# Cross-attention with image prompts: a column read in place, a key chunk and a sum moved in the last batch

## The chip, the cores and the metric

The kernel runs on one core of one Trainium2 chip. Its time is device microseconds of one launch, the median of several runs. The core's engines are TensorE (PE in the profile; PEld is its weight load), VectorE (DVE), ScalarE (ACT), GpSimd (POOL) and SyncE (SP), which issues the transfers. Each works through its own queue of instructions in order and waits on semaphores for the others.

## The reference

For 8 batches of 112 queries with 320 channels (20 heads of 16) there are 371 text keys and 4 prompt keys, each a row of 512. The core of what is computed:

```python
q = heads(hidden_states @ W_q); k_t = heads(text_ehs @ W_k); v_t = heads(text_ehs @ W_v)
probs_t = softmax(q k_t * scale);  text_out = probs_t v_t
attn_scores = q k_ip * scale
qsem = l2norm(probs_t @ text_ehs);  sem = qsem @ l2norm(ip_ehs)
probs_ip = softmax(attn_scores + 0.5 * sem) * spatial_mask
out = (text_out + probs_ip v_ip) @ W_out + b_out + hidden_states
```

All is float32.

## The kernel before, in words

The length of qsem isn't taken from qsem itself: with the Gram matrix G of the text rows, its square is p G p. So each batch builds a matrix u (L426, L506) that holds G in blocks of 32 rows, the products with the normalised prompts, a column of ones and the values of the heads at hand. For each head, `multiplied` (L574 on) forms p u in 12 steps j of four matmuls, one for each of the four heads of a group (L587). From the result's PSUM banks, ACT copies the last 21 columns into pvs (`value_sums`, L600): 4 prompt products, the sum of p (column NIP) and 16 value sums. `reduced` (L625) multiplies the first 371 columns by p and sums them on DVE, which gives the squared length, ss. In the last batch two of a group's four heads go another way: `shared` copies the bank on ACT (L610), multiplies on POOL (L614) and sums on ACT (L618).

The heads of a batch are worked on in five groups g = 0 to 4. `scores` (L540) and `probabilities` (maximum on DVE L553, exponential on ACT L557, transfer into the ring xg) run two groups ahead of `multiplied`; `transposed` (L568) turns the ring into xgT one group ahead. `placed` (L506, on POOL) puts the values of the next group's heads into u, in three pieces, each as soon as PE is done with that piece of the group before.

`keys` makes the transposed keys kT in three chunks of 128 channels (L448, copied at L455). Groups 0 and 1 need the first chunk, groups 2 and 3 the second, group 4 the third. In the last batch (b = 7) the third chunk is made after the products of group 1 (L941).

`finish` is a generator that takes a batch from pvs and ss to the output in pieces, so that its pieces can be set between other work: the sum with the bias xb (L659, POOL); z, the sum of p, copied out of pvs (L661), z2 = z * z * eps * eps and rn = max(ss, z2) (L664, L666); the root (L669, between two loads of ACT tables) and attn = values / z (L675, POOL); the fused prompt scores fu (L680 to L686); their exponential ex (L690); sums and weights w (L696 to L700, DVE), and in the same piece the weighted prompt values wv (L702), their fold (L713) and two additions to attn (L714, L715), all four on POOL; the transpose of attn (L721) and its copy aT (L725); the product with W_out (L734); the addition of xb (L743); the transfer out (L746). The last batch is finished in two parts: heads 0 to 15 (`first`) while group 4 is multiplied, heads 16 to 19 (`last`, late=True, on DVE where others use POOL) at the very end. `awake` issues matmuls on a unit matrix whose result nobody reads (ps_w, L371).

The orders of PE, SP, DVE and (after the prologue) ACT are those of the source. POOL's order isn't: a scheduler of the framework decides it at build time, from when it expects operands to be ready. The last batch is written out by hand from L907 to L962. PSUM has three pools: four banks for products (ps_qd), two for scores (ps_sc) and two for the rest (ps_mm), given out in turn; in the last batch heads 0 and 1 of the groups from 2 on take their scores' banks from ps_mm, as the key chunk does.

Of the kernel before, what the change touches and what calls it, by code (L numbers as in the profile page):

```python
# [8 lines left out]
F32 = mybir.dt.float32  # L9
# [5 lines left out]
NIP = 4  # L15
# [5 lines left out]
def kernel(  # L21
# [14 lines left out]
    nc = tc.nc  # L36
# [327 lines left out]
    def awake(n, end=False):  # L364

        if end:
            ps = ps_qd.tile([P, 512], F32, tag="qd", name=f"ps_w_{n}")
        else:
            ps = bank(f"ps_w_{n}", spare=True)
        for _ in range(n):  # L370
            nc.tensor.matmul(ps[:, :P], ident, ident, start=True, stop=True)  # L371
# [266 lines left out]
    def finish(b, heads=(0, H), eng=None, late=False, table=None):  # L638


        s = st[b]
        eng = eng or nc.gpsimd
        h0, h1 = heads
        n = h1 - h0
        part = slice(h0, h1)

        def sm(name):
            return small.tile([S, H], F32, tag=name, name=f"{name}_{b}_{h0}", bufs=1)[:, :n]

        def sm4(name):  # L650
            return small.tile([S, H, NIP], F32, tag=name, name=f"{name}_{b}_{h0}", bufs=1)[:, :n]

        def over_ip(t):
            return t.unsqueeze(2).to_broadcast([S, n, NIP])

        pvs = s["pvs"][:, part]
        if not late:
            s["xb"] = work.tile([S, C], F32, tag="xb", name=f"xb_{b}", bufs=1)
            nc.gpsimd.tensor_tensor(s["xb"], x_sb[:, b, :], bias_sb, ALU.add)  # L659
        z = sm("z")  # L660
        nc.vector.tensor_copy(z, pvs[:, :, NIP])  # L661

        z2 = sm("z2")
        nc.vector.scalar_tensor_tensor(z2, z, EPS * EPS, z, ALU.mult, ALU.mult)  # L664
        rn = sm("rn")
        nc.vector.tensor_tensor(rn, s["ss"][:, part], z2, ALU.max)  # L666
        yield

        nc.scalar.activation(rn, rn, AF.Sqrt)  # L669
        nc.scalar.preload_act_table(AF.Exp)  # L670
        zr = sm("zr")
        nc.vector.reciprocal(zr, z)
        attn = attn_ring[b % 2]
        ah = attn[:, :C].rearrange("p (h d) -> p h d", d=D)[:, part]
        eng.tensor_tensor(  # L675
            ah, pvs[:, :, NIP + 1 :], zr.unsqueeze(2).to_broadcast([S, n, D]), ALU.mult
        )
        yield

        nc.vector.reciprocal(rn, rn)  # L680
        fu = sm4("fu")
        nc.vector.tensor_tensor(fu, pvs[:, :, :NIP], over_ip(rn), ALU.mult)
        nc.vector.scalar_tensor_tensor(fu, fu, SEM_SCALE, s["ipl"][:, part], ALU.mult, ALU.add)
        mx = sm("mx")
        nc.vector.tensor_reduce(mx, fu, AX.X, ALU.max)
        nc.vector.tensor_tensor(fu, fu, over_ip(mx), ALU.subtract)  # L686
        yield

        ex = sm4("ex")
        nc.scalar.activation(ex, fu, AF.Exp)  # L690
        if table:
            nc.scalar.preload_act_table(table)
        yield

        sx = sm("sx")
        nc.vector.tensor_reduce(sx, ex, AX.X, ALU.add)  # L696
        rx = sm("rx")
        nc.vector.reciprocal(rx, sx)
        w = sm4("w")
        nc.vector.scalar_tensor_tensor(w, ex, sm_sb, over_ip(rx), ALU.mult, ALU.mult)  # L700
        wv = work.tile([S, NIP, H, D], F32, tag="wv", name=f"wv_{b}_{h0}", bufs=1)[:, :, :n]
        eng.tensor_tensor(  # L702
            wv,
            s["vip"][:, :, part],
            w.rearrange("p h n -> p n h").unsqueeze(3).to_broadcast([S, NIP, n, D]),
            ALU.mult,
        )
        if late:
            ips = small.tile([S, GROUP, D], F32, tag="ips", name=f"ips_{b}", bufs=1)
            nc.vector.tensor_reduce(ips, wv.rearrange("p n h d -> p h d n"), AX.X, ALU.add)  # L710
            nc.vector.tensor_tensor(ah, ah, ips, ALU.add)
        else:
            eng.tensor_tensor(wv[:, :2], wv[:, :2], wv[:, 2:], ALU.add)  # L713
            eng.tensor_tensor(ah, ah, wv[:, 0], ALU.add)  # L714
            eng.tensor_tensor(ah, ah, wv[:, 1], ALU.add)  # L715
        yield

        i0, i1 = h0 * D // P, -(-h1 * D // P)
        ps = bank(f"ps_a_{b}_{h0}", spare=True)
        for i in range(i0, i1):  # L720
            nc.tensor.transpose(  # L721
                ps[:, i * S : (i + 1) * S], attn[:, i * P : (i + 1) * P], ident[:S, :S]
            )
        aT = work.tile([P, NC, S], F32, tag="aT", name=f"aT_{b}_{h0}")
        nc.scalar.copy(  # L725
            aT[:, i0:i1], ps[:, i0 * S : i1 * S].rearrange("p (i s) -> p i s", s=S)
        )
        yield

        if not late:  # L730
            s["o"] = bank(f"ps_o_{b}", spare=b >= B - 2)
        ps = s["o"]
        for i in range(i0, i1):
            nc.tensor.matmul(  # L734
                ps[:S, :C], aT[:, i, :], wo_sb[:, i, :], start=(i == 0), stop=(i == NC - 1)
            )
        if h1 < H:
            yield
            return
        yield  # L740

        ob = work.tile([S, C], F32, tag="ob", name=f"ob_{b}", bufs=1)
        nc.vector.tensor_tensor(ob, ps[:S, :C], s["xb"], ALU.add)  # L743
        yield

        nc.sync.dma_start(out[b], ob)  # L746
        del st[b]
        yield
# [12 lines left out]
    def run(key, make, pieces=1):  # L761

        if key not in gens:
            gens[key] = make()
        for _ in range(pieces):
            next(gens[key], None)

    def between(b, g):

        nb = b + 1  # L770
        new = nb < B


        first = [bs for bs in pairs if bs[0] == (nb if b == 0 else nb + 1)]
        rest = [bs for bs in pairs if bs[0] == nb]
        if g == 0:
            if new:
                run(("g", nb), lambda: gram(nb), 3)
            if b == 0:
                run(("pp",), prompt_projections, NC + 1)  # L780
            if b > 0:
                run(("f", b - 1), lambda: finish(b - 1))
        if g == 1:
            if new:
                run(("v", nb), lambda: values(nb), 2)
            for bs in first if b == 0 else ():
                run(("q", bs[0]), lambda: project_queries(bs), 3)
        if g == 2 and new:
            run(("v", nb), None)
            run(("k", nb), lambda: keys(nb))  # L790
            for bs in first if b == 0 else ():
                run(("q", bs[0]), None)
        if g == 2 and b > 0 and new:
            run(("f", b - 1), None)
        if g == 3:
            if new:
                run(("k", nb), None, 1)
            for bs in first if b > 0 else ():
                run(("q", bs[0]), lambda: project_queries(bs), 3)
            run(("t", b), lambda: prompt_logits(b))  # L800
            if nb < B - 1:
                run(("k", nb), None, 1)
            if b > 0 and new:
                run(("f", b - 1), None)
            for bs in rest:
                run(("q", bs[0]), None)
        if g == 4:
            if nb + 1 < B:
                run(("c", nb + 1), lambda: transposed_context(nb + 1))
            if b > 0 and new:  # L810
                run(("f", b - 1), None, 2)
            if nb + 1 < B:
                run(("c", nb + 1), None, 2)
            for bs in (first if b > 0 else []) + rest:
                run(("q", bs[0]), None)
# [94 lines left out]
    for g in range(NG):  # L910
# [7 lines left out]
        for j, _ in enumerate(multiplied(b, g)):  # L918
            for a in {0: (2, 3), 1: (0, 1)}.get(j, ()) if g == 0 else ():
                scores(b, coming, a)  # L920
                probabilities(b, coming, a)
            if j == 2 and g + 1 < NG:
                transposed(b, g + 1)
            if j == 2 and g == 1:
                run(before, None, 3)
# [12 lines left out]
            run(("f", b - 2), None)  # L938
        if g == 1:
            prompt_values(b)  # L940
            run(("k", b), None)  # L941
        between(b, g)
        if g == 2:
            run(before, None)
        if g == 3:

            first = finish(b, (0, FULL * HC), table=AF.Sqrt)
            for _ in range(5):
                next(first)
    last = finish(b, (FULL * HC, H), nc.vector, late=True)  # L950
    run(before, None, 2)
    awake(14, end=True)
    for _ in range(3):
        next(last)
    run(before, None)
    next(last)
    next(first)
    next(first)
    run(before, None)
    drain(first)  # L960
    awake(2, end=True)
    drain(last)  # L962


# [41 lines left out]
```

## Time and profile before

| what | value |
|---|---|
| median of 3 runs (lowest, highest) | 456.55 us (455.42, 456.96) |
| the profiled execution: its time, its span | 457.1 us, 455.3 us |
| PE busy | 440.5 us, 97% |
| DVE, ACT, POOL busy | 313.7, 188.8, 113.3 us |
| mean granted clock of PE | 0.991 |
| last batch: first product to last instruction | 401.4 to 455.3 us |

The profile is of one execution. Times in it are us from the start of the span. A row of the timeline gives the start, the duration, the engine, the line and operation, the tile written and the tiles read (numbers left out), their shapes, how many instructions are merged into the row, and in brackets for how long the engine had been idle and what ended that. PEclk is the clock that was granted to PE, as a share of the full one. Each float32 matmul of the source appears as two in the trace.

### The profile page before, as it was taken

What the parts mean: (1) busy time and instruction counts of PE and PEld (TensorE: products, weight loads), DVE (VectorE), ACT (ScalarE), POOL (GpSimd) and SP (SyncE); (2) the same over time, 40 slices, a digit from 0 to 9 for tenths busy, and PEclk for the clock granted to TensorE, in tenths of its full rate; (3) what the DMA queues carried; (4) which work ended last, traced back from release to release, by engine and by line L of the source; (5) the groups of instructions that cost most, each with busy time, mean ns of one, the idle gap of its engine ahead of it and who ended that gap; (6) DMA issues with size and microseconds to landing.
All of it is one profiled execution on the core that took longest, in us unless ns stands there. A gap on an engine that the chain in (4) does not pass through costs nothing. (4 is left out here: it accounts for less than half of the span.)

```text
span 455.3 us, 12992 instructions
## 1 busy us (share of the span) xinstructions
PE 440.5 (97%) x5146; PEld 340.1 (75%) x5146; DVE 313.7 (69%) x670; ACT 188.8 (41%) x523; POOL 113.3 (25%) x262
## 2 busy tenths in 40 slices
PE   8998999999999999999999999999999999998976
PEld 8757867877678877887678777888777877875854
DVE  4047276786677768787686768787686768888854
ACT  2264233345334353345335353435344353346532
POOL 4302200102051113222060212311150212323570
PEclk9999999999999999999999999999999999999989
DMA  8669954645646554545645555545645445654200
GB/s 238 181 167 252 201 134 136 150 128 163 161 125 160 142 139 140 140 138 158 170 119 141 153 156 145 139 125 151 170 125 131 140 114 157 148 146 138 61 1 25
DMA packets 52068, 64.99 MB, mean 143 GB/s; under 512 B 18368, under 2 KB 43984, under 8 KB 52008
## 3 DMA queue, kind: packets, MB, share of 16 engines
q1 hardware_dynamic: 51568, 63.62, 53.1%
q8 instruction: 40, 0.66, 0.7%
q10 hardware_dynamic: 440, 0.56, 0.4%
q14 instruction: 20, 0.16, 0.1%
HBM read 19.46 MB, written 5.12 MB: 54 GB/s over the span
## 5 line engine op out<-in xcount | busy, mean ns | idle before, releaser
L587 PE MATMUL ps_qd<-u,xgT 32*112 32x232 f32 (+11 forms) x3840 | 220.9, 356 | 4.2 <-POOL u L506 3.8
L587 PEld LDWEIGHTS ps_qd<-u,xgT 32*112 32x112 f32 x3840 | 185.0, 173 | 42.4 <-issue 10.9
L553 DVE TENSOR_REDUCE nmx<-ps_s 112x1 f32<-112x371 f32 x160 | 77.6, 528 | 68.7 <-PE ps_s L540 68.0
L568 DVE STREAM_TRANSPOSE xgT<-xg 128x1536 f32<-128x1536 f32 x40 | 118.9, 2972 | 7.3 <-DMA xg<-p 7.3
L557 ACT ACTIVATE p<-ps_s,nmx 112x371 f32<-112x371 f32 x160 | 82.5, 573 | 62.6 <-DVE nmx L553 46.7
L625 DVE CUSTOM_DVE_ANT_0 junk<-ps_qd,p 112x371 f32<-112x371 f32 x154 | 83.5, 542 | 22.5 <-ACT pvs L600 5.7
L506 POOL COPY u<-vr 128x64 f32<-128x64 f32 x120 | 26.1, 240 | 169.4 <-PE ps_qd L587 113.4
L540 PE MATMUL ps_s<-kT,qm 32*112 32x371 f32 x320 | 62.9, 480 | 2.4 <-ACT kT L455 2.1
L465 PE MATMUL ps_v<-wv_sb,ctxT 128*128 128x384 f32 (+1 forms) x192 | 63.5, 480 | 0.0
L465 PEld LDWEIGHTS ps_v<-wv_sb,ctxT 128*128 128x128 f32 x192 | 35.2, 190 | 19.7
L448 PE MATMUL ps_k<-ctxT,wk_sb 128*128 128x371 f32 x144 | 48.7, 482 | 0.0
L600 ACT COPY pvs<-ps_qd 112x21 f32<-112x21 f32 x160 | 16.5, 189 | 72.6 <-PE ps_qd L587 72.6
L448 PEld LDWEIGHTS ps_k<-ctxT,wk_sb 128*128 128x128 f32 x144 | 26.5, 190 | 16.1 <-issue 0.5
L412 PE MATMUL ps_g<-ctxT 128*128 128x375 f32 (+2 forms) x168 | 37.4, 379 | 0.0
L412 PEld LDWEIGHTS ps_g<-ctxT 128*128 128x128 f32 x168 | 28.1, 190 | 8.4
L540 PEld LDWEIGHTS ps_s<-kT,qm 32*112 32x112 f32 x320 | 25.1, 170 | 7.3 <-ACT kT L455 4.7
L310 DVE TENSOR_SCALAR qm<-ps_q,emask 128x224 f32<-128x224 f32 (+1 forms) x25 | 9.2, 400 | 25.1 <-PE ps_q L301 25.1
L702 POOL TENSOR_TENSOR wv<-vip,w 112x1280 f32<-112x1280 f32 (+1 forms) x8 | 19.2, 2405 | 17.0 <-DVE w L700 14.8
L472 ACT COPY vext<-ps_v 128x384 f32<-128x384 f32 (+1 forms) x24 | 11.2, 466 | 24.9 <-PE ps_v L465 24.4
L455 ACT COPY kT<-ps_k 128x371 f32<-128x371 f32 x18 | 8.5, 472 | 27.3 <-PE ps_k L448 27.3
L400 ACT ACTIVATE ug<-ps_g 128x375 f32<-128x375 f32 (+2 forms) x24 | 9.0, 377 | 23.5 <-PE ps_g L412 19.0
L401 POOL TENSOR_TENSOR ug<-ug,half 128x128 f32<-128x128 f32 (+1 forms) x24 | 10.7, 448 | 29.9 <-ACT ug L400 29.9
(111 smaller groups left out, 323.2 us busy)
## 6 DMA issues: line engine op xcount, KB each, us to landing
xg<-p SPq DMA_DIRECT2D x160, 162.3 KB
u<-ug SPq DMA_DIRECT2D x128, 99.0 KB
vip<-vipd SPq DMA_DIRECT2D x8, 560.0 KB
ct<-in_ctx_dram SPq DMA_DIRECT2D x16, 256.0 KB
vr<-vd SPq DMA_DIRECT2D x32, 120.0 KB
vd<-vext SPq DMA_DIRECT2D x7, 320.0 KB
ct<-in_ctx_dram SPq DMA_DIRECT2D x8, 224.0 KB
vd<-vext SPq DMA_DIRECT2D x7, 160.0 KB
```

The costliest lines, as they stand in the source:

```text
L412: nc.tensor.matmul(ps[:, : T - t0], ctxT[:, e, t0 : t0 + P], ctxT[:, e, t0:T], start=(e == 0), stop=(e == NE - 1),)
L448: nc.tensor.matmul(ps[:, :TT], wk_sb[:, e, i * P : (i + 1) * P], s["ctxT"][:, e, :TT], start=(e == 0), stop=(e == NE - 1),)
L465: nc.tensor.matmul(ps[:, :w], ctxT[:, e, c * P : (c + 1) * P], wv_sb[:, e, :w], start=(e == 0), stop=(e == NE - 1),)
L506: nc.gpsimd.tensor_copy(region(b, c)[:, :, UV - c * P :], s["vr"][:, c * QN : (c + 1) * QN, g, :])
L540: nc.tensor.matmul(ps[:S, :TT], qm[a * RG : (a + 1) * RG, i, r, j * S : (j + 1) * S], s["kT"][a * RG : (a + 1) * RG, i, :], start=True, st ...
L553: nc.vector.tensor_reduce(nmx, ps[:S, :TT], AX.X, ALU.max, negate=True)
L557: nc.scalar.activation(p, ps[:S, :TT], AF.Exp, bias=nmx)
L568: nc.vector.transpose(xT.rearrange("p j (k q) -> p q j k", q=QN), xg.rearrange("p q (j k) -> p q j k", k=RG),)
L587: nc.tensor.matmul(banks[a][:S, j * RG : UW], xT[a * RG : (a + 1) * RG, j, :S], region(b, c)[a * RG : (a + 1) * RG, q, q * RG :], start=(j ...
L600: nc.scalar.copy(s["pvs"][:, h, :], ps[:S, TT:UW])
L625: nc.vector.tensor_tensor_reduce(out=junk, in0=ps[:S, :TT], in1=s["p", g][:, a, :], scale=1.0, scalar=0.0, op0=ALU.mult, op1=ALU.add, accu ...
L702: eng.tensor_tensor(wv, s["vip"][:, :, part], w.rearrange("p h n -> p n h").unsqueeze(3).to_broadcast([S, NIP, n, D]), ALU.mult,)
```

## The change

It has five edits, all in the arrangement, none in what is computed.

- In `finish`, z is no longer copied; column NIP of pvs is read in place by z2 and by the reciprocal.
- In the last batch xb takes its memory from the buffers named ctxT (which hold the transposed context and later the tile of `shared`) and not from the single buffer xb.
- `finish` gives up control once more, between w and wv. The calls are adapted: group 2 of other batches runs two pieces where it ran one; for batch 6, w stays at group 2 of the last batch, and wv with what follows is issued after the value columns of group 4.
- The third chunk of the last batch's keys is issued inside the products of group 1, after step j = 1.
- In the tail, 11 keep-awake matmuls replace 14, the last two go, and the transpose of `first` with its copy aT is issued ahead of the exponential ex of `last`.

```diff
         if not late:
-            s["xb"] = work.tile([S, C], F32, tag="xb", name=f"xb_{b}", bufs=1)
+            if b == B - 1:
+                s["xb"] = work.tile([P, NE, TP], F32, tag="ctxT", name=f"xb_{b}")[:S, 0, :C]
+            else:
+                s["xb"] = work.tile([S, C], F32, tag="xb", name=f"xb_{b}", bufs=1)
             nc.gpsimd.tensor_tensor(s["xb"], x_sb[:, b, :], bias_sb, ALU.add)
-        z = sm("z")
-        nc.vector.tensor_copy(z, pvs[:, :, NIP])
+        z = pvs[:, :, NIP]
...
         nc.vector.scalar_tensor_tensor(w, ex, sm_sb, over_ip(rx), ALU.mult, ALU.mult)
+        yield
...
         if g == 2 and b > 0 and new:
-            run(("f", b - 1), None)
+            run(("f", b - 1), None, 2)
...
+            if j == 1 and g == 1:
+                run(("k", b), None)
             if j == 2 and g + 1 < NG:
                 transposed(b, g + 1)
...
         if g == 1:
             prompt_values(b)
-            run(("k", b), None)
         between(b, g)
         if g == 2:
             run(before, None)
         if g == 3:
+            run(before, None)
             first = finish(b, (0, FULL * HC), table=AF.Sqrt)
-            for _ in range(5):
+            for _ in range(6):
                 next(first)
     last = finish(b, (FULL * HC, H), nc.vector, late=True)
     run(before, None, 2)
-    awake(14, end=True)
+    awake(11, end=True)
     for _ in range(3):
         next(last)
     run(before, None)
+    next(first)
     next(last)
-    next(first)
     next(first)
     run(before, None)
     drain(first)
-    awake(2, end=True)
     drain(last)
```

## The prediction

> **What bounds the kernel now.** I read the page first. TensorE (PE) is busy nearly all the time, at full clock but for two slices near the end.
>
> ```profile
> PE 440.5 (97%) x5146; PEld 340.1 (75%) x5146; DVE 313.7 (69%) x670; ACT 188.8 (41%) x523; POOL 113.3 (25%) x262
> PEclk9999999999999999999999999999999999999989
> ```
>
> Every edit that acts before the last batch only shortens VectorE (DVE) there, so the question is the last batch (404 us to the end). The busy times by 1 us stretch (columns: stretch, length, busy PE, PEld, DVE, ACT, POOL, granted clock, DMA) show its two holes:
>
> ```profile
> 418.00:419.00 1.00, 0.00 (x0) 0.00 (x0) 0.75 (x3) 1.00 (x5) 0.40 (x1) 1.00 1.01 297
> 421.00:422.00 1.00, 1.00 (x9) 0.46 (x8) 1.00 (x3) 1.00 (x3) 0.00 (x0) 0.50 0.00 0
> 433.00:434.00 1.00, 0.00 (x0) 0.00 (x0) 0.85 (x3) 0.17 (x1) 0.92 (x2) 1.00 0.00 0
> 438.00:439.00 1.00, 1.00 (x12) 0.69 (x8) 0.76 (x3) 1.00 (x1) 0.00 (x0) 0.50 0.00 0
> ```
>
> PE stands still at 418 and 433, and each time runs at clock 0.50 some microseconds later. The timeline (start, duration, engine, line, tiles) says why:
>
> ```profile
> 409.61 1.00 DVE L661 COPY z<-pvs 112x20 f32<-112x20 f32 x1
> 410.64 0.18 DVE L664 SCALAR_TENSOR_TENSOR z<-z 112x20 f32<-112x20 f32 x1
> 410.95 1.89 DVE L553 TENSOR_REDUCE nmx<-ps_s 112x1 f32<-112x371 f32 x4
> 411.58 1.96 ACT L557 ACTIVATE p<-ps_s,nmx 112x371 f32<-112x371 f32 x4 [2.61 <-POOL shared L614]
> 414.46 2.76 PE L448 MATMUL ps_k<-ctxT,wk_sb 128*128 128x371 f32 x8
> 418.74 0.52 ACT L455 COPY kT<-ps_k 128x371 f32<-128x371 f32 x1
> 419.31 1.05 PE L540 MATMUL ps_s<-kT,qm 32*112 32x371 f32 x8 [2.09 <-ACT kT L455]
> 429.41 2.47 POOL L702 TENSOR_TENSOR wv<-vip,w 112x1280 f32<-112x1280 f32 x1 [0.17 <-DVE w L700]
> 435.32 0.61 POOL L506 COPY u<-vr 128x64 f32<-128x64 f32 x3
> 435.61 6.49 PE L587 MATMUL ps_qd<-u,xgT 32*112 32x392 f32 x96 [2.70 <-POOL u L506]
> ```
>
> First hole, 2.09 us: the third key chunk is made after group 1's products, and its copy kT stands on ACT behind two table loads and group 1's evacuation. Second hole, 2.70 us: the value columns u of group 4 stand on POOL behind wv, its fold and two additions of batch 6. The tail after group 4 (442.10) is a chain too:
>
> ```profile
> 444.77 3.29 PE L371 MATMUL ps_w<-ident 128*128 128x128 f32 x28
> 446.99 0.21 ACT L690 ACTIVATE ex<-fu 112x16 f32<-112x16 f32 x1
> 448.29 0.35 ACT L725 COPY aT<-ps_a 128x224 f32<-128x224 f32 x1 [1.08 <-PE ps_a L721]
> 450.30 0.26 PE L721 MATMUL ps_a<-ident,attn 112*128 112x112 f32 x1
> ```
>
> **What the Trainium skill says.** "TensorE: Matmul & The Clock Gate", Part 1: the clock is halved after an idle activity window of about 3.4 us, and the window runs free, so the same kernel meets it at different phases. The trace agrees: 0.50 from about 420.0 to 423.4 and from 437.0 to 440.3. "SBUF — State Buffer", Who interferes with whom: a DVE instruction with two SBUF inputs and a GpSimd instruction that reads SBUF exclude each other, the later one blocks. The trace agrees: with a POOL multiplication from 155.24 to 155.70, z2 (L664) started at 155.41 and ended at 155.74, 0.33 us in place of 0.18. For the rest no page is needed.
>
> **The change part by part.** All sums are against the profiled execution (457.1 us, span 455.3, so 1.8 us lie around it); it stands 0.55 us above the median of 456.55.
>
> *Score column in place.* Nine copies go. Those of batches 0 to 5 took about 0.17 us each under PE work (58 to 60 us busy in each 60 us stretch): nothing; were that cover gone, 6 x 0.2 = 1.2 us. Batch 6's took 1.00 us at 409.61, since POOL's second multiplication (L614) held the port until 410.58. The next instruction, z2, has two SBUF inputs, so I take it that it now waits there itself until 410.62; only 0.17 + 0.04 = 0.21 us are won for the maxima and exponentials behind it. Other bound: z2 isn't blocked, and the first exponential moves to 410.65, where its own wait for POOL ends: 0.93 us. The first of batch 7 (0.54 us at 434.87) leads to POOL's attention of its heads 0 to 15, ready at 444.01, 3.9 us ahead of its transpose: nothing. The second (0.16 us at 444.89) stands ahead of ex, which gets another wait (below): nothing.
>
> *Third chunk inside the products.* The built order puts its four matmuls behind steps j = 0 and 1 of group 1. The chunk's PSUM bank is the one of scores (group 3, head 0), so it waits for that exponential, the third of four at 0.46 us: 412.50 to 413.07, after the change 412.86. PE gets there at 410.45, where j = 2 started before. So PE waits 2.45 us, with ten steps of group 1 queued behind. Then 2.76 us of chunk and the rest of group 1 (414.46 - 410.45 = 4.01): group 1 ends at 412.90 + 6.77 = 419.67. Scores of group 4, formerly 419.31, start then, 0.36 us later. kT now precedes the table loads on ACT (copy done 416.2, loads, root and exponential 3.3 us more: 419.6), just in time for the evacuation.
> Before, group 2 found its banks long free. Now it starts on group 1's heels, and waits for its copies and sums as group 1 did behind group 0, whose products end at 407.87: from one end to the next 414.46 - 407.87 = 6.59 us. Group 2 ends at 426.26 at full clock; it was 426.48, of which half clock cost 6.36 - (5.71 - 0.42) = 1.07.
> Half clock: about 2.2 us of PE idling inside a 3.4 us window is what both holes before had (2.1), so it likely strikes again, now on the chunk and group 1. Cost between 1.07 (measured on products) and 1.7 (half of 3.4 on dense matmuls); I take 1.5: 427.76, against before +1.28. Without it -0.22.
>
> *Batch 6's sums "behind" the value columns.* They are issued later in the source, but POOL's order isn't written by hand, and in the built program wv, fold and additions still stand ahead of u. The second hole stays whole, with its half clock.
>
> *xb.* It leaves POOL's end (447.20 to 448.06, off the path) for a place between the value columns of group 3 and the multiplications of group 2: it runs 426.97 to 427.83 by the old clock, so these start 0.5 us later than 427.32 and end at 429.78, and wv, waiting for them and for w, starts at about 429.9: +0.5 (bounds 0.39 and 0.55), straight into group 4's start. Its new buffer waits for sums of ACT that ended at 423.9: nothing.
>
> *Tail.* 3 of 14 keep-awake matmuls go: 6 x 0.1175 = 0.70 us, and 0.61 us of the last two. But aT of the first 16 heads now precedes ex on ACT: PE ends ps_w at 447.36, aT takes 447.58 to 447.93, ex ends at 448.19 in place of 447.20, and the chain from it to attn (2.27 us, less 0.15 for xb gone from POOL) at 450.35; the last transpose starts at 450.5, it was 450.30: +0.2 (bounds -0.7, if that chain shrinks as well, and +0.6, if PE cools down while it waits). No DMA is added; SP's order is the same.
>
> Sum: 1.28 + 0.5 + 0.2 = +2.0: 459.1 as profiled, 458.5 beside the median.
>
> **Rivals.** (1) No half clock: the wait straddles two windows. Then -0.22 + 0.5 + 0.2 = +0.5: 457.0, not slower by what can be told. For it: free phase, and runs before that spread over 1.5 us. Against: both holes before struck. It decides below some 1.5 to 2 us of idling in one window. (2) The lock isn't taken: the wait shrinks by 0.72 to 1.7 us, too short for half clock; -0.22 - 0.72 + 0.7 = -0.2: 456.3. Against: z2 at 155.41. (3) The change does what it says on POOL: u right behind group 3, group 4 at 432.9 in place of 435.6, no half clock: -2.7 - 1.1, a later attention of batch 7 gives back 0.5: about 453.5. Against: the built order.
>
> **How the numbers follow.** A measurement of this kernel can tell about 0.3% (1.4 us) from no change: 455.2 to 457.9. Forecast 0.52, nearly all of it above 457.9; rival 1 0.28; rival 2 0.08; rival 3 0.07; something unseen 0.05. Slower 0.50, same 0.38, faster 0.12. The range runs from rival 2 (456.2) to the forecast with the full 1.7 us, xb's upper bound and a cooled tail (459.6), leaving out rival 3 and the unseen. The forecast's own range is 457.5 to 459.6.
>
> **What would show it.** Right: a PE hole of about 2.4 us at 410.5 ahead of ps_k, clock 0.50 behind it, no hole before the scores, wv still ahead of u, the hole of about 3 us before group 4, ex behind aT. Wrong: exponentials of group 3 from 410.7, full clock throughout group 1, or u ahead of wv.

## The result: 459.01 us, 0.55% longer

| kernel | median | lowest, highest | runs | profiled execution: time, span, mean clock of PE |
|---|---|---|---|---|
| before | 456.55 us | 455.42, 457.23 | 9 | 457.1, 455.3, 0.991 |
| after | 459.01 us | 457.33, 459.82 | 9 | 459.82, 458.0, 0.983 |

The ratio is 1.0055, with a 95% interval from 1.0039 to 1.0071. The forecast was 458.5.

The profiled execution of after is the slowest of its nine and one of two with a mean clock of 0.983. Six of the nine had 0.989 or 0.990, hardly less than the 0.991 of before's profiled execution. So the trace of after shows more time at half clock than most of its executions had, and its account must be read with that in mind.

The page of after, its busy times and its clock by slices:

```profile
PE 442.0 (96%) x5136; PEld 339.3 (74%) x5136; DVE 311.4 (68%) x661; ACT 188.4 (41%) x523; POOL 113.1 (25%) x262
PEclk9999999999999999999999999999999999997979
```

PE has ten records less than before and is busy 1.5 us longer: its work did not grow, it ran more slowly. Of the last four slices two stand at 7 in the clock's row; before, the lowest was a single 8. The busy times by 1 us stretch (columns as before) show where:

```profile
411.00:412.00 1.00, 0.00 (x0) 0.00 (x0) 1.00 (x3) 1.00 (x3) 0.00 (x0) 0.88 0.00 0
...
414.00:415.00 1.00, 1.00 (x2) 0.44 (x2) 1.00 (x2) 0.00 (x0) 0.00 (x0) 0.50 0.63 183
...
436.00:437.00 1.00, 0.00 (x0) 0.00 (x0) 0.83 (x3) 0.00 (x0) 0.92 (x2) 0.50 0.00 0
...
440.00:441.00 1.00, 1.00 (x12) 0.60 (x8) 0.54 (x2) 1.00 (x1) 0.19 (x1) 0.50 0.00 0
```

There are still two holes. The first has moved from 418 to 411, the second is at the same place of the program, ahead of group 4. The timeline of after, the rows that answer to those of before:

```profile
409.07 1.00 DVE L667 SCALAR_TENSOR_TENSOR z<-pvs 112x20 f32<-112x20 f32 x1
410.11 0.18 DVE L669 TENSOR_TENSOR rn<-ss,z 112x20 f32<-112x20 f32 x1
410.20 1.89 DVE L553 TENSOR_REDUCE nmx<-ps_s 112x1 f32<-112x371 f32 x4
410.82 1.95 ACT L557 ACTIVATE p<-ps_s,nmx 112x371 f32<-112x371 f32 x4 [2.42 <-POOL shared L614]
...
412.37 5.31 PE L448 MATMUL ps_k<-ctxT,wk_sb 128*128 128x371 f32 x8 [1.64 <-ACT p L557]
...
417.72 0.47 ACT L455 COPY kT<-ps_k 128x371 f32<-128x371 f32 x1 [3.96 <-PE ps_k L448]
...
421.43 0.86 PE L540 MATMUL ps_s<-kT,qm 32*112 32x371 f32 x8
...
428.41 0.87 POOL L663 TENSOR_TENSOR xb<-x_sb,bias_sb 112x320 f32<-112x320 f32 x1
...
431.32 2.47 POOL L707 TENSOR_TENSOR wv<-vip,w 112x1280 f32<-112x1280 f32 x1 [0.18 <-DVE w L703]
...
437.23 0.64 POOL L506 COPY u<-vr 128x64 f32<-128x64 f32 x3
...
437.54 7.22 PE L587 MATMUL ps_qd<-u,xgT 32*112 32x392 f32 x96 [3.13 <-POOL u L506]
```

Read it from the bottom of the first hole: the key chunk (ps_k) is released by an exponential (p, L557), not by its operands, and its eight matmuls take 5.31 us where they took 2.76. Row z is now the instruction z2 itself, and it takes the 1.00 us that the copy took. The scores no longer wait for kT. On POOL wv still stands ahead of u, and group 4 still waits for u, longer than before, and then takes 7.22 us where it took 6.49. The tail of after:

```profile
447.43 2.62 PE L371 MATMUL ps_w<-ident 128*128 128x128 f32 x22
...
450.28 0.34 ACT L730 COPY aT<-ps_a 128x224 f32<-128x224 f32 x1 [0.82 <-PE ps_a L726]
450.52 0.22 ACT L693 ACTIVATE ex<-fu 112x16 f32<-112x16 f32 x1
...
453.05 0.29 PE L726 MATMUL ps_a<-ident,attn 112*128 112x112 f32 x1 [1.04 <-DVE attn L716]
```

The exponential ex stands behind aT, and the last transpose waits 1.04 us for attn.

Where the 2.7 us between the two spans lie can be added up from the starts of ACT's copies pvs (L600), which follow the end of each group's products at once:

| stretch | before | after | difference |
|---|---|---|---|
| start of the span to the copies of group 0 | 407.81 | 407.26 | -0.55 |
| copies of group 0 to copies of group 2 | 18.65 | 20.70 | +2.05 |
| copies of group 2 to the first product of group 4 | 9.15 | 9.58 | +0.43 |
| group 4, first product to its copies | 6.51 | 7.25 | +0.74 |
| those copies to the end of the span | 13.18 | 13.21 | +0.03 |
| span | 455.3 | 458.0 | +2.7 |

In this execution half clock lasted two stretches of 3.4 us at each hole of the last batch; before had one at each. Of the kernels below that keep the chunk at this place, four had one stretch on it (e2, e6, e7, e9): for them the second row is 19.36 to 19.73, that is +0.7 to +1.1. With the +0.43 of the third row this makes +1.1 to +1.5 for an execution with one stretch at each hole. What else belongs to the 2.46 us between the medians no trace shows.

### The profile page after: what moved, and what is told of

It reads as the page before. It is cut to its first block, busy times and chain, and to the rows that moved or that the text cites. A ratio compares the mean times of both kernels' runs of the same rounds, so it can differ in the third digit from the quotient of the medians.

```text
span 458.0 us, 12965 instructions
## 1 busy us (share of the span) xinstructions
PE 442.0 (96%) x5136; PEld 339.3 (74%) x5136; DVE 311.4 (68%) x661; ACT 188.4 (41%) x523; POOL 113.1 (25%) x262
## 4 chain that ended last, share of the span: by engine, by line
PE 91%; ACT 3%; POOL 2%; DMA 2%; DVE 1%; issue 1%; SPq 0%; DVEq 0%; ACTq 0%
PE ps_qd L587 42%; PE ps_v L465 14%; PE ps_k L448 10%; PE ps_g L412 8%; PE ps_s L540 4%; PE ps_q L301 3%; PE ps_o L739 3%; PE ps_c L351 2%; ACT p L557 1%; PE ps_g L384 1%; DMA xg<-p 1%; PE ps_w L371 1%; DMA ct<-in_ctx_dram 1%; PE ps_a L726 1%; PE ps_ip L517 1%
## 5 line engine op out<-in xcount | busy, mean ns | idle before, releaser
L587 PE MATMUL ps_qd<-u,xgT 32*112 32x168 f32 (+11 forms) x3840 | 221.5, 356 | 4.8 <-POOL u L506 4.3
L557 ACT ACTIVATE p<-ps_s,nmx 112x371 f32<-112x371 f32 x160 | 82.4, 572 | 64.0 <-DVE nmx L553 48.3
L448 PE MATMUL ps_k<-ctxT,wk_sb 128*128 128x371 f32 x144 | 51.3, 502 | 1.6 <-ACT p L557 1.6
L600 ACT COPY pvs<-ps_qd 112x21 f32<-112x21 f32 x160 | 16.4, 188 | 71.5 <-PE ps_qd L587 71.4
L448 PEld LDWEIGHTS ps_k<-ctxT,wk_sb 128*128 128x128 f32 x144 | 27.6, 197 | 19.2 <-ACT p L557 2.2
```

The lines of the kernel that those rows point to most:

```text
L448: nc.tensor.matmul(ps[:, :TT], wk_sb[:, e, i * P : (i + 1) * P], s["ctxT"][:, e, :TT], start=(e == 0), stop=(e == NE - 1),)
L557: nc.scalar.activation(p, ps[:S, :TT], AF.Exp, bias=nmx)
L587: nc.tensor.matmul(banks[a][:S, j * RG : UW], xT[a * RG : (a + 1) * RG, j, :S], region(b, c)[a * RG : (a + 1) * RG, q, q * RG :], start=(j ...
L600: nc.scalar.copy(s["pvs"][:, h, :], ps[:S, TT:UW])
```

## The experiments

The theory to test: the loss is the wait of the chunk for its PSUM bank, with half clock behind it, not the chunk's new place as such, and the other edits give nothing or cost a little. The first rival was that the other edits (xb, the tail) make the loss; the second, that the chunk costs by standing inside the products, wait or no wait. None of these kernels leaves out or changes a part of the computation. "0 to 2" is the stretch from the copies of group 0 to those of group 2, in us, in the profiled execution. The ratios are to runs of before beside them, whose medians were 456.70 to 456.90 us (456.55 for after). They are worked out from the single runs and can differ from the quotient of two medians by up to 0.15%.

| kernel | median | ratio to before, 95% interval | chunk: wait, duration | 0 to 2 | group 4: wait, duration |
|---|---|---|---|---|---|
| before | 456.55 | | none, 2.76 | 18.65 | 2.70, 6.49 |
| after | 459.01 | 1.0055 [1.0039, 1.0071] | 1.64, 5.31 | 20.70 | 3.13, 7.22 |
| e1 chunk back | 456.64 | 1.0012 [0.9992, 1.0032] | none, 2.76 | 16.76 | 3.08, 6.49 |
| e2 chunk alone | 458.63 | 1.0040 [1.0021, 1.0059] | 1.84, 4.45 | 19.73 | 2.69, 6.49 |
| e3 chunk after j = 6 | 455.66 | 0.9977 [0.9965, 0.9989] | none, 2.76 | 16.43 | 3.11, 6.40 |
| e4 other bank | 456.69 | 0.9998 [0.9983, 1.0014] | 0.72, 2.76 | 16.93 | 3.13, 7.59 |
| e5 POOL by hand | 458.38 | 1.0039 [1.0024, 1.0055] | 2.25, 5.32 | 21.28 | 1.13, 7.00 |
| e6 ex first | 457.59 | 1.0013 [0.9997, 1.0030] | 1.65, 4.27 | 19.36 | 3.11, 6.34 |
| e7 xb back | 457.96 | 1.0030 [1.0017, 1.0044] | 1.66, 4.46 | 19.54 | 2.69, 6.49 |
| e8 maxima first | 456.70 | 1.0000 [0.9980, 1.0021] | 0.87, 2.76 | 17.06 | 3.12, 7.41 |
| e9 hole filled | 457.28 | 1.0015 [1.0001, 1.0028] | 1.66, 4.46 | 19.54 | 0.59, 4.80 |
| e10 column alone | 456.43 | 0.9994 [0.9972, 1.0017] | none, 2.76 | 18.52 | 2.69, 6.49 |
| e11 repaired | 453.61 | 0.9924 [0.9900, 0.9947] | none, 2.76 | 15.98 | 0.56, 4.80 |
| e12 repaired, POOL by hand | 453.54 | 0.9933 [0.9911, 0.9955] | none, 2.76 | 15.96 | 0.97, 5.77 |

### Which edit makes the loss

**e1: after, with the chunk back behind the products of group 1.**

```diff
-            if j == 1 and g == 1:
-                run(("k", b), None)
...
             prompt_values(b)
+        if g == 1:
+            run(("k", b), None)
```

> The changed kernel, but the third key chunk stands behind group 1's products again, as before the change. Theory (the chunk's wait on its bank inside group 1 and the half clock behind it make the loss): what remains is xb's 0.43 us in front of wv and up to 0.7 us of half clock in group 4, so 457.0 to 457.8, 0.5 to 1.2 us above before, and a first hole ahead of the scores of about 2 us as before. Rival (xb, the column read in place or the tail make the loss): stays at about 459.0, 2.5 us above before.

**e2: before, with the move of the chunk alone.**

```diff
+            if j == 1 and g == 1:
+                run(("k", b), None)
...
             prompt_values(b)
-            run(("k", b), None)
```

> The kernel before with only the third key chunk moved behind step j = 1 of group 1. Theory: this edit alone makes most of the loss, 1.3 to 2.1 us, so 457.9 to 458.7; PE waits about 2 us ahead of ps_k and the chunk runs at half clock. Rival (the other edits make it): within 0.5 us of before.

The timeline of e2 at the chunk:

```profile
413.58 4.45 PE L448 MATMUL ps_k<-ctxT,wk_sb 128*128 128x371 f32 x8 [1.84 <-ACT p L557]
```

The move alone makes 0.40% [0.21%, 0.59%] of the 0.55%, and with it undone no difference from before can be told. So the chunk is the main part, the other edits together make no difference that can be told, and the first rival falls. e1 came out 0.4 us below what was expected: in its profiled execution the old hole ahead of the scores was there (1.88 us), but no half clock followed it, so that 0 to 2 took 16.76 us and not 18.65.

### The wait, or the place

**e3: after, with the chunk after step j = 6,** where the exponentials of group 3 are done.

```diff
-            if j == 1 and g == 1:
+            if j == 6 and g == 1:
```

> The changed kernel with the chunk behind step j = 6 of group 1 and not j = 1. By then the exponential that frees its bank has ended, so theory: no wait ahead of ps_k, no half clock in group 1; kT stands behind ex on ACT and the scores of group 4 wait about 1 us; group 2 ends about 1.4 us earlier than before, less 0.43 for xb and up to 0.7 for half clock in group 4: 455.5 to 456.3. Rival (a chunk inside the products costs by itself, since group 2 then starts on group 1's heels): 457.5 or more.

**e4: after, with the chunk in a bank of the scores' pool,** which the first and not the third of the four exponentials sets free.

```diff
-            ps = bank(f"ps_k_{b}_{i}")
+            ps = bank(f"ps_k_{b}_{i}", spare=b == B - 1 and i == FULL)
```

> The changed kernel with the chunk's PSUM bank taken from the scores' pool, whose next bank is freed by the first of the four exponentials and not by the third, 0.93 us earlier. Theory: the hole ahead of ps_k shrinks from 1.6 to about 0.7 us, too short for half clock: 455.9 to 456.6; if half clock strikes all the same, about 458. Rival (the wait on the bank is not what costs): stays at about 459.

**e8: after, with the first piece of batch 6's finish (z2 among it) issued behind group 3's maxima,** so that these don't stand behind z2.

```diff
-            if b > 0:
+            if 0 < b < B - 1:
                 run(("f", b - 1), lambda: finish(b - 1))
...
             probabilities(b, coming, a)
+        if g == 1:
+            run(before, lambda: finish(b - 1))
         drain(sums)
```

> The changed kernel with z2 and rn of batch 6 behind the four maxima of group 3 on DVE and not ahead of them. Theory (z2 waits for POOL's multiplications, and the maxima wait behind it): z2 falls from 1.00 to about 0.2 us, the first exponential starts 0.7 us earlier, right when POOL ends, and the hole ahead of ps_k is about 0.9 us and not 1.64; 456.5 to 458.3, by whether half clock still strikes. Rival (reading the column with a stride makes z2 slow): z2 stays near 1 us and the time at 459 or below by no more than 0.7.

The timeline of e3 at the chunk and at the scores of group 4:

```profile
413.26 2.76 PE L448 MATMUL ps_k<-ctxT,wk_sb 128*128 128x371 f32 x8
...
417.89 0.89 PE L540 MATMUL ps_s<-kT,qm 32*112 32x371 f32 x8 [0.62 <-ACT kT L455]
```

The timeline of e4 at the chunk:

```profile
411.79 2.76 PE L448 MATMUL ps_k<-ctxT,wk_sb 128*128 128x371 f32 x8 [0.72 <-ACT p L557]
```

The timeline of e8, z2 and the chunk:

```profile
410.76 0.18 DVE L667 SCALAR_TENSOR_TENSOR z<-pvs 112x20 f32<-112x20 f32 x1
...
411.48 2.76 PE L448 MATMUL ps_k<-ctxT,wk_sb 128*128 128x371 f32 x8 [0.87 <-ACT p L557]
```

All three leave the chunk inside the products and shorten its wait, in three different ways: to nothing, to 0.72, to 0.87 us. In all three the chunk runs at full clock (2.76 us), 0 to 2 is 3.6 to 4.3 us shorter than in after, and the loss is gone. The second rival falls: inside the products the chunk costs nothing as long as its bank is free. With it at j = 6 the kernel is even 0.23% [0.11%, 0.35%] faster than before; PE then waits 0.62 us for kT. e8 also shows where the wait comes from: z2 takes 0.18 us as soon as POOL isn't multiplying at that moment, and the maxima and exponentials move up. e4 ended 0.1 us above what was expected, with two stretches of half clock on group 4 (7.59 us).

### The other edits

**e10: before, with the score column in place alone.** `z = pvs[:, :, NIP]` replaces tile and copy.

> The kernel before with only the score column read in place. Theory (z2 waits in the copy's place, the other copies lie under PE work): the same time within 0.3 us, 456.5. Rival (the copies were on the path): 1 us or more faster, 455.5 or less. Other rival (the strided column is slow to read): slower by 0.3 us or more.

**e7: after, with xb in its single buffer again,** in the last batch too.

> The changed kernel with xb of the last batch in its own single buffer again, so that it stands at POOL's end. Theory: shared multiplications and wv start 0.43 us earlier, the hole before group 4 is 2.7 us and not 3.1, 458.6, half clock apart. Rival (xb lies under other waits): hole unchanged.

**e6: after, with ex of the last heads ahead of aT of the first sixteen,** as before had it.

```diff
     run(before, None)
-    next(first)
     next(last)
     next(first)
+    next(first)
```

> The changed kernel with the exponential of the last four heads ahead of aT of the first sixteen on ACT, as before the change. Theory (aT in front of ex is why the shorter keep-awake stretch won nothing): ex runs about 1 us earlier after group 4, the last transpose waits for PE's own work and not for attn, and the tail from the end of group 4 to the end of the span shrinks from 13.2 us to about 12.3: 458.1. Rival (the tail is bound by PE or the transfer out): 13.2 us and 459.0.

The timeline of e7 at group 4:

```profile
436.75 6.49 PE L587 MATMUL ps_qd<-u,xgT 32*112 32x392 f32 x96 [2.69 <-POOL u L506]
```

The timeline of e6 at ex and the last transpose:

```profile
447.25 0.22 ACT L693 ACTIVATE ex<-fu 112x16 f32<-112x16 f32 x1
...
449.78 0.29 PE L726 MATMUL ps_a<-ident,attn 112*128 112x112 f32 x1
```

e10 is what was expected: no difference, and z2 takes 1.01 us in it. e7 takes the second hole back from 3.13 to 2.69 us: xb ahead of the multiplications costs 0.44. Its median alone, 457.96, couldn't have told this; its interval overlaps that of after. In e6 the last transpose waits for nothing, and from the copies of group 4 (442.57) to the end of the span (454.8) it takes 12.23 us, where after takes 13.21; the interval of e6 lies below that of after. That aT went ahead of ex costs this microsecond. It takes back what the tail had won on before's 13.18: the missing keep-awake matmuls can be the reason for that gain, but e6 also has the column in place and xb's new place, and the three weren't separated here.

### The second hole

**e5: after, with POOL's order, too, kept as written in the last batch,** so that the value columns really stand ahead of batch 6's sums. This fixes the place of all of POOL's other work of the batch as well.

```diff
+    ctx.enter_context(
+        tc.manual_schedule(
+            engines=engines | {mybir.EngineType.Activation, mybir.EngineType.Pool}
+        )
+    )
     b = B - 1
```

> The changed kernel with POOL's order in the last batch that of the source, so that wv and what follows for batch 6 really stands behind the value columns of group 4. Theory (the sums ahead of u make the second hole): the 3.13 us hole before group 4 and its half clock (1.2 to 1.9 us) go; POOL is then later with batch 7's attention, by about 1.2 us behind the keep-awake matmuls, and ex behind aT carries that on: 455.0 to 456.3, some 3.3 us under the changed kernel. Rival (u itself waits on PE, or another engine sets group 4): the hole stays and the time is about 459.

The timeline of e5:

```profile
409.53 1.02 DVE L667 SCALAR_TENSOR_TENSOR z<-pvs 112x20 f32<-112x20 f32 x1
410.44 0.86 POOL L663 TENSOR_TENSOR xb<-x_sb,bias_sb 112x320 f32<-112x320 f32 x1
410.58 0.76 DVE L669 TENSOR_TENSOR rn<-ss,z 112x20 f32<-112x20 f32 x1
...
433.51 2.93 DVE L568 STREAM_TRANSPOSE xgT<-xg 128x1536 f32<-128x1536 f32 x1 [1.64 <-DMA xg<-p]
...
434.90 0.24 POOL L506 COPY u<-vr 128x64 f32<-128x64 f32 x1 [0.52 <-PE ps_qd L587]
...
435.09 2.46 POOL L707 TENSOR_TENSOR wv<-vip,w 112x1280 f32<-112x1280 f32 x1
...
436.59 7.00 PE L587 MATMUL ps_qd<-u,xgT 32*112 32x392 f32 x96 [1.13 <-DVE xgT L568]
...
440.27 0.90 DVE L686 SCALAR_TENSOR_TENSOR fu<-fu,ipl 112x64 f32<-112x64 f32 x1
```

This missed by over 2 us. The order is now as the change describes it, and the hole shrinks from 3.13 to 1.13 us. But the wait is replaced: group 4 now stands on the transpose of its probabilities, which itself waits 1.64 us for their transfer. Half clock comes all the same, and group 4 takes 7.00 us. The third cost is on DVE: batch 6's sums on POOL now lie under batch 7's prompt scores, whose two-input instructions have to wait (fu 0.90 us; it took 0.22 in after). And the first hole grew by the same edit: as written, xb of batch 6 comes right behind POOL's multiplications (410.44; in after it ran at 402.35), rn takes 0.76 us beside it and not 0.18, and the maxima and exponentials behind rn are late. The first exponential starts 4.15 us after the copies of group 0 and not 3.56, and the chunk waits 2.25 us and not 1.64. So e5 changes both holes, and its time alone doesn't tell what the sums' place is worth.

**e9: after, with 11 keep-awake matmuls ahead of group 4,** which add work but no dependence: `awake(11)` where g is 3, in front of batch 6's last pieces.

> The changed kernel with 11 more keep-awake matmuls on PE right ahead of group 4, about 2.6 of the 3.1 us of its second hole. Theory (an idle stretch costs twice, as itself and as half clock behind it): the hole as a span stays, but group 4 runs at full clock, 5.3 us in place of 6.5 to 7.2, so 457.1 to 457.8, some 1.2 to 1.9 us under the changed kernel. Rival (the clock follows something else, such as the load after the hole): no change, 459.

The timeline of e9:

```profile
434.31 2.70 PE L371 MATMUL ps_w<-ident 128*128 128x128 f32 x22
...
437.61 4.80 PE L587 MATMUL ps_qd<-u,xgT 32*112 32x392 f32 x96 [0.59 <-POOL u L506]
```

u comes no earlier and group 4 starts at the same place, but it takes 4.80 us and not 7.22: 2.4 us of after's profiled execution is half clock behind the second hole. The median is 1.7 us below that of after.

### Together

**e11: after with the edits of e3, e8, e6 and e9. e12: after with those of e3, e8, e6 and e5,** no filling, and xb of batch 7 issued behind the additions to attn.

> The changed kernel with the chunk behind step j = 6, the maxima of group 3 ahead of z2, ex ahead of aT and the second hole filled with 11 keep-awake matmuls. Theory: these repairs add up, from the 455.7 of the chunk behind j = 6: 0.9 us in the tail, up to 0.6 from the wait of kT, 1.1 from group 4's clock: 453.0 to 454.2. Rival (they remove the same wait): 455 or more.

> As the kernel before it, but without the filling, with POOL's order in the last batch that of the source and xb at its end. Theory: the second hole shrinks from 3.1 to about 1.1 us, then bound by the transfer of group 4's probabilities, and batch 7's attention on POOL comes about 1 us after the keep-awake matmuls: 452.5 to 454.5. Rival (POOL's later attention gives all of it back): 455 or more.

The timeline of e11 at group 4:

```profile
433.24 4.80 PE L587 MATMUL ps_qd<-u,xgT 32*112 32x392 f32 x96 [0.56 <-POOL u L506]
```

The timeline of e12 at the same place:

```profile
430.88 5.77 PE L587 MATMUL ps_qd<-u,xgT 32*112 32x392 f32 x96 [0.97 <-DVE xgT L568]
```

Both are faster than before (ratios 0.9924 and 0.9933, intervals in the table), over 5 us below after by their medians, and can't be told apart. e12 ends group 4 1.4 us earlier, and gives this back: its ps_w takes 3.75 us at half clock where e11's takes 2.62, and its first product with W_out waits 1.59 us for aT. Beside e11 POOL's written order does no harm here, where z2 and rn stand behind the maxima and the chunk doesn't wait. That points to the chunk's wait, 0.6 us of which came from that order, as what kept e5 above before; e12 differs from e5 in more than this, so it isn't shown. Which of the four edits in e11 makes how much of its gain wasn't separated.

## Why the prediction was right: its steps against the runs

The mechanism was the forecast's: a bank wait on the chunk, half clock on it, no gain from POOL's order. That the sum came so close is in part luck: its terms were off by up to 1.5 us, and in opposite directions. Step by step:

- **Column in place, 0.21 us won.** Right. From the copies of group 0 to the first exponential it is 3.77 us before (407.81 to 411.58) and 3.56 after (407.26 to 410.82). The Trainium skill's "SBUF — State Buffer", Who interferes with whom, was the basis (a DVE instruction with two SBUF inputs and a POOL instruction that reads SBUF shut each other out), and the traces agree: 1.00 us for z2 beside POOL's multiplication, 0.18 in e8 behind it. The rival in which the lock isn't taken is out.
- **The chunk's wait.** Right in its place, its cause and its end: 412.90 was expected by before's clock, 5.09 us after the copies of group 0, and it is 5.11. The length wasn't: PE was to stand still from 2.64 us after those copies, for 2.45 us, but the last product ahead of the chunk ends after 3.47 us (410.73), so the hole is 1.64 us. The prediction counted from where the next product would have started, the trace from where the last one ended.
- **Group 2 without half clock, -0.22.** Too pessimistic. e8, whose wait is 0.77 us shorter than after's, needs 17.06 us from 0 to 2; with after's wait that would be 17.8, so -0.8. I let the ten steps behind the chunk take 4.01 us as before, but having waited they find their banks free and take 3.54 (e4, e8).
- **Half clock, 1.5 us (bounds 1.07 and 1.7).** The term that was mis-sized. In after it is 5.31 - 2.76 on the chunk and 3.99 - 3.54 on the products behind it: 3.0 us, since it lasted from about 411.8 to 418.6, two stretches and not one. With one stretch (e2: 4.45 - 2.76 on the chunk) it is 1.7, the upper bound. Rival 1, no half clock, would have been near e4 and e8. By the prediction's own measure it should have come true: it was to decide below some 1.5 to 2 us of idling in one window, and in after PE had idled 1.03 us (410.73 to 411.76) when the clock fell. That the clock fell all the same wasn't foreseen by that rule. The error of this term and the one above go against each other: +2.05 in place of +1.28.
- **POOL's order.** Right: wv, fold and additions ahead of u. Rival 3 failed as the change stands, and e5 shows that writing POOL's order by hand doesn't bring its 453.5 either (458.38; that order also makes the chunk wait longer).
- **xb, +0.5.** +0.43 between the copies of group 2 and group 4, 0.44 by e7.
- **Group 4's products.** Not in the sum, and they cost +0.74: half clock lasted from about 435.6 to 442.5, again two stretches where before had one. The longer hole alone doesn't make this: e1, e3 and e6, with holes of 3.08 to 3.11 us, had one (6.34 to 6.49 us). The prediction had the hole and its half clock right, but booked the latter as unchanged.
- **Tail, +0.2.** +0.03. ex ended 5.95 us after the copies of group 4 (450.74), 0.87 later than before (447.20, after 5.08); 0.99 was expected.
- The -0.55 ahead of the last batch is a difference between two executions, not shown to be the change's.

- **The range.** Its upper end, 459.6, isn't the sum of what it names: 458.5 + 0.2 (half clock) + 0.05 (xb) + 0.4 (tail) is 459.2. The median lies below both.

The sum as profiled was 459.1, and 459.8 was measured, in the slowest of the nine; the median is 459.01 against 458.5.

## What to carry to other kernels

Work that is moved into a dense stretch takes its buffer with it: ask what frees that buffer at the new place, and put it behind the release (j = 6 cost nothing, j = 1 cost 0.4%). A PE hole of a few microseconds has two prices, the wait and the half clock behind it, and the second can be taken away without the first (e9). An order in the source is an order on the chip only on engines whose order is written by hand: look for it in the built program before any time is booked on it.

## What the runs showed of the hardware that was not expected

How long half clock lasts. The busy times of after behind the first hole:

```profile
415.00:416.00 1.00, 1.00 (x3) 0.68 (x2) 0.01 (x1) 0.00 (x0) 0.74 (x1) 0.50 0.67 184
...
418.00:419.00 1.00, 1.00 (x16) 0.61 (x16) 0.00 (x0) 0.98 (x2) 0.00 (x0) 0.71 0.20 67
```

And those of e6 there:

```profile
412.00:413.00 1.00, 0.62 (x1) 0.50 (x2) 1.00 (x2) 1.00 (x3) 0.00 (x0) 0.53 0.06 16
...
415.00:416.00 1.00, 1.00 (x4) 0.66 (x3) 0.01 (x1) 0.00 (x0) 0.74 (x1) 0.77 0.64 177
```

A clock of 0.88 in the stretch from 411 (above) puts the fall in after at about 411.76, and 0.71 the return at about 418.58: 6.8 us. In e6 0.53 and 0.77 put them at 412.06 and 415.46: 3.4 us. PE idled until 412.37 and 412.38, so the first 3.4 us at half clock held 0.61 us of idling in after and 0.32 in e6. The other places where I worked this out fit: 0.65 us (chunk of e5), 1.1 and 1.5 (group 4 of e4 and e8) and 1.9 (group 4 of after) gave two stretches, 0.13 us (group 4 of e3) and none at all (chunk of e2) gave one. So a hole that goes on for 0.6 us or more past the fall doubles the price of half clock, and which it is depends on phase: the same chunk took 5.31 us in after and 4.27 in e6, which differ only behind it. The Trainium skill's "TensorE: Matmul & The Clock Gate", Part 1, has the stretch (3.4 us) and that a busy one brings the clock back; that as little as 0.6 us of idling makes it not count as busy is a reading of these runs.

The page gives as the rule for kernels that there be no idle gaps above some 3.4 us (HAM oscillation), and the prediction took from its Part 1 that an idle window halves the clock. The runs don't bear that out: in none of the stretches of 3.4 us worked out here, ahead of a fall, was PE idle throughout. Holes of 1.64 to 3.13 us brought half clock here, and 1.13 us in e5, and often the clock fell before the hole was over: after 1.03 us of it at the chunk of after, and after 1.24 of 3.13 us at its group 4. Waits of 0.56 to 0.97 us (e3, e4, e8, e11, e12) did not bring it. But the length of the hole doesn't decide: 1.88 us ahead of the scores of e1 brought none. And far from any such hole, early in the kernel, the clock of e1 fell from 28.8 to 32.2 us (and that of e2 from 28.6 to 32.0), where PE had idled 0.35 us in the 3.4 us before. It is the 8 among the first slices of e1's page, where before has a 9:

```profile
PEclk9989999999999999999999999999999999999988
```

What else counts, the work around the hole among it, stays open.
